# Class biases in four column tiles, vectors laid ready as operands, and a first block in a set order of TensorE

## The chip, the cores and the metric

The kernel runs on one core of a Trainium2 chip. Its time is the device time of one execution in microseconds (us). The kernel before took 2043.91 us, the median of three runs (2043.42 to 2048.09). The profile shows one further execution. The engines are named as in the profile: PE is TensorE, with PEld for its weight loads; DVE is VectorE, ACT is ScalarE, POOL is GpSimd, and SP is SyncE, which here only issues DMAs.

## The reference

Two sequences (B = 2) of 2048 tokens with 512 channels go through three stages, each of which takes the one before as its input:

```python
y   = cond(x, cond_512)                    # a modulated 512x512 linear, clipped
x   = x + attn(y)                          # gated linear recurrence, then a gated MLP with down projection
x   = x + ffn(cond2(x, ids, states))       # six branches, an MLP of two layers, an int8 product
```

The change lies at the seam between the second and the third. What matters there is the first layer of `cond2`:

```python
h = _ln(x, pw_g[pathway_ids], pw_b[pathway_ids]); h = _ln(h, cp_g[compartment_ids], cp_b[compartment_ids])
t = _ln(x, tm_g[time_steps], tm_b[time_steps])
m = x + _mlp_ln(memory_state, ...);  n = x + _mlp_ln(noise_state, ...);  r = x + _mlp_ln(resource_state, ...)
s = _ln(x, ms_g[scale_type], ms_b[scale_type])
cat = concatenate([w[0]*h, w[1]*t, w[2]*m, w[3]*n, w[4]*r, w[5]*s])     # 6 x 512 columns
return _mlp_ln(cat, int_W1, int_b1, int_W2, int_b2, int_g, int_be)      # silu(cat @ int_W1 + b1) @ int_W2 ...
```

Three facts make this cheaper than six products of 512x512. The branches m, n and r all hold the same x plus one vector per sequence, so the blocks of `int_W1` that belong to them are added up, and the three vectors times their blocks become a bias. The ids of a token take few values (5, 3 and 2 classes, 10 in all), so what the additive halves of the class tables contribute after `int_W1` is a table of 10 biases of 512 numbers; a token's own row is picked by a matmul with its one-hot vector. The multiplicative halves (gains) are picked in the same way and multiplied in.

## The kernel before

**Down projection.** The MLP's down projection (`down`) runs over four super-blocks of 1024 tokens. Each is a product of 1536 by 512 in Strassen-Winograd form with seven part products, which `paired_in_place` (L174) sets out: it keeps four quarters of the input, B11, B21, B12, B22, and replaces them by their differences in place (`sums`, L201, DVE). Each part product is a step of PE matmuls (`product`, L129, the matmul at L132): `dn_a` with B11, `dn_b` with B21, `dn_d` with B22 and again with the changed B11, then `dn_a` with the changed B22, with B12 and with B21. One fp32 matmul is two instructions in the records of PE. The changed B22 comes from a difference on DVE, which has to be there before its `dn_a`. Results are added to the residual (L818 and L826 on DVE) and stored. `then` hangs further work behind a step.

**Weights of the third stage.** While the last super-block runs, `int_W1` is made ready. Blocks 3 and 4 lie whole in `int_w_3` and `int_w_4` (`raw`, L1101), blocks 2 and 1 in quarters in two tiles `w_int` (`quarters`, L1107); each block is scaled by its softmax weight (`scaled`, L1083, the scaling at L1085 on DVE). Behind step 1, `vectors_and_x` (L1127) does the following. `vectors` (L1087) multiplies the three vectors by blocks 2, 3 and 4: 12 matmuls of 32 columns by 512, which are put into four column tiles, each with an operand of 128x32 that is set to zero (L1094) and filled by a copy of two columns (L1095) on DVE; four such buffers take turns. The result is copied to `bias` (L1099). POOL adds blocks 3 and 4 onto block 2 (L1131), makes the combinations that the seven products need (`combine`, L119 to L124), and SP loads blocks 5 and 0 (L1115) into the two buffers that blocks 3 and 4 leave; DVE scales them, POOL combines them.

**First block of the third stage.** The third stage works on 8 blocks of 512 tokens. `by_tokens` (L1251) turns x to tokens in rows (`tr_x`, L1266; `tr_oh` for one-hot vectors, L1276), computes layer norms, gathers the rows of `pw` by index (L1246, POOL), multiplies and adds (L1291, L1292) and normalises again; `by_channels` (L1301) turns the normed x (`tr_l`) and the branch h (`tr_h`) back (L1226, with an ACT copy at L1229) to `lnT` and `hT`; `gains` (L1308) picks the gains by a matmul (L1318) and multiplies on DVE (L1323): `tT` and `lnT` both come from `lnT`, then `hT` is multiplied in place. `up` (L1329) then is again `paired_in_place`, with the quarters made of `x2T`, `lnT`, `tT` and `hT`; its banks are `ps_h_a`, `ps_h_b`, `ps_h_d`. `added` (L1359) adds each token's row of the bias table to three of its results.

**Class bias.** Ahead of the first block the table of biases is made (L1498 to L1521): one matmul that brings the sum of the vectors in (L1501), 8 matmuls with an operand of 10 columns (`betas`) in `ps_bias` (L1504) and 4 in `ps_bias_s` (L1510), all 512 long and one behind the other. DVE adds them up (L1517 to L1520), POOL's `split` (L997) cuts the sum into three bf16 parts, and SP stores these as `tables` (L1004).

**Order.** Outside an order written by hand, a scheduler places the instructions of each engine by its own estimates and priorities; once placed, each engine's queue runs in its order, and a waiting instruction holds up all that stand behind it. `tc.manual_schedule` sets an engine's order as written, and `issue_after` puts an instruction behind another on its queue. The gathers of the second block are queued behind the last copy of `split`.

## Time and profile before

| What | us |
|---|---|
| Median of three runs (lowest, highest) | 2043.91 (2043.42, 2048.09) |
| The profiled execution, by its own time | 2045.46 |
| Its span in the profile | 2043.7 |
| PE busy | 2016.0 |
| `ps_vec` and the four dn_d instructions among it | 1341.57 to 1351.20 |
| Class bias on PE, 26 instructions | 1403.86 to 1415.11 |
| First block, from there to its last `added` | 1415.11 to 1443.05 |
| DVE, ACT, POOL busy | 1195.5, 653.2, 157.9 |

The span is the time between the first and last instruction that the profile shows; 1.76 us lie around it. Times along the span count from its start. A timeline lists, for one engine, start and length of groups of like instructions, and in brackets how long the engine had been idle before them and what ended that. The length of a group of PE instructions includes the drain of the last one, so the next can start some 0.17 us before it ends. PEclk is the share of the full TensorE clock that was granted.

### The profile page before, as it was taken

To read this page: it belongs to the slowest core of one execution; us is meant where nothing else is said; L and a number is where in the kernel's file an instruction comes from. 1 tells how busy PE (TensorE), PEld (TensorE's weight loads), DVE (VectorE), ACT (ScalarE), POOL (GpSimd) and SP (SyncE) were. 2 spreads that over 40 slices of the span, in tenths; PEclk is the share of its full clock that TensorE was granted. 3 is DMA by queue.
4 is the path that set the end of the run, shared out by engine and by line. 5 is a ranking of instruction groups with operands and counts; after the bars stand their busy time and mean duration, and the time that the engine had idled before them with its cause. 6 is when DMAs were issued, how large, how long until landed. Compare 5 with 4: busy or idle time off the path is not lost.

```text
span 2043.7 us, 17016 instructions
## 1 busy us (share of the span) xinstructions
PE 2016.0 (99%) x6374; PEld 1067.9 (52%) x6374; DVE 1195.5 (58%) x1798; ACT 653.2 (32%) x861; POOL 157.9 (8%) x126
## 2 busy tenths in 40 slices
PE   8999999999999999999999999999999999999997
PEld 4444444444444444444444444434877777777774
DVE  6766666667533324234325475476588678678675
ACT  4547777776422222222221000001302302302301
POOL 1420000012100000000010000072000000000000
PEclk9999999999999999999999999999999999999999
DMA  6731213232212212111335766624111111111000
GB/s 214 260 136 52 83 52 95 60 113 82 93 42 76 78 41 93 41 42 52 102 116 179 225 223 216 220 94 165 41 43 62 60 45 62 61 43 62 21 21 21
DMA packets 83971, 193.54 MB, mean 95 GB/s; under 512 B 6544, under 2 KB 34742, under 8 KB 79792
## 3 DMA queue, kind: packets, MB, share of 16 engines
q1 hardware_dynamic: 79280, 175.67, 25.3%
q0 software_dynamic: 4608, 16.78, 2.5%
q8 instruction: 50, 0.82, 0.2%
q14 instruction: 33, 0.27, 0.0%
HBM read 133.27 MB, written 58.75 MB: 94 GB/s over the span
## 4 chain that ended last, share of the span: by engine, by line
PE 93%; DVE 4%; DMA 1%; issue 1%; ACT 0%; SPq 0%; DVEq 0%; ACTq 0%
PE up_a L132 16%; PE ps_h_a L132 11%; PE rec_a L132 10%; PE up_d L132 8%; PE dn_a L132 7%; PE ps_h_d L132 6%; PE rec_d L132 5%; PE ps_o L1397 5%; PE up_b L132 4%; PE dn_d L132 4%; PE ps_h_b L132 3%; PE rec_b L132 3%; PE y_a L132 2%; PE dn_b L132 2%; PE ps_f L1421 1%; PE y_d L132 1%
## 5 line engine op out<-in xcount | busy, mean ns | idle before, releaser
L132 PE MATMUL up_a<-h,w_up 128*128 128x512 f32 x384 | 172.6, 592 | 0.0
L132 PE MATMUL dn_a<-op,w_dn 128*128 128x512 f32 x384 | 167.4, 594 | 0.0
L699 DVE SCALAR_TENSOR_TENSOR prod<-up_d,cols,k 128x512 f32<-128x512 f32 x48 | 36.0, 751 | 200.7 <-ACT k L265 200.7
L265 ACT COPY k<-up_a 128x512 f32<-128x512 f32 x144 | 84.2, 585 | 195.4 <-PE up_a L132 195.4
L679 ACT ACTIVATE gate<-gate,cols 128x512 f32<-128x512 f32 x96 | 68.8, 721 | 218.3 <-DVE gate L678 218.3
L132 PE MATMUL up_a<-h2T,w_up 128*128 128x512 f32 x288 | 129.5, 592 | 0.0
L132 PEld LDWEIGHTS up_a<-h,w_up 128*128 128x128 f32 x384 | 72.9, 190 | 91.9 <-issue 89.7
L132 PEld LDWEIGHTS dn_a<-op,w_dn 128*128 128x128 f32 x384 | 72.2, 190 | 88.8 <-issue 86.5
L132 PE MATMUL rec_a<-hT,w_rec 128*128 128x512 f32 x256 | 115.6, 593 | 1.1 <-ACT k L265 1.1
L132 PE MATMUL rec_a<-h,w_rec 128*128 128x512 f32 x256 | 115.1, 592 | 0.0
L1397 PE MATMUL ps_o<-int_w,h 128*128 128x512 f32 x224 | 103.6, 605 | 0.0
L132 PEld LDWEIGHTS up_a<-h2T,w_up 128*128 128x128 f32 x288 | 54.7, 190 | 68.9 <-issue 68.9
L132 PE MATMUL up_d<-h,w_up 128*128 128x512 f32 x192 | 87.5, 599 | 0.0
L132 PE MATMUL up_b<-h,w_up 128*128 128x512 f32 x192 | 86.3, 592 | 0.0
L132 PE MATMUL dn_d<-op,w_dn 128*128 128x512 f32 x192 | 84.2, 595 | 0.0
L132 PEld LDWEIGHTS rec_a<-hT,w_rec 128*128 128x128 f32 x256 | 48.5, 190 | 63.0 <-issue 60.3
L132 PEld LDWEIGHTS rec_a<-h,w_rec 128*128 128x128 f32 x256 | 48.6, 190 | 61.2 <-issue 61.2
L265 ACT COPY k<-rec_a 128x512 f32<-128x512 f32 x96 | 55.7, 580 | 70.2 <-PE rec_a L132 70.0
L678 DVE TENSOR_TENSOR gate<-up_b,k 128x512 f32<-128x512 f32 x48 | 32.9, 690 | 76.1 <-PE up_b L132 74.7
L132 PE MATMUL up_d<-h2T,w_up 128*128 128x512 f32 x144 | 65.2, 592 | 0.0
L1397 PEld LDWEIGHTS ps_o<-int_w,h 128*128 128x128 f32 x224 | 40.2, 189 | 46.5 <-issue 46.5
L132 PE MATMUL ps_h_a<-tT,w_int 128*128 128x256 f32 x256 | 64.2, 385 | 0.0
(389 smaller groups left out, 3475.4 us busy)
## 6 DMA issues: line engine op xcount, KB each, us to landing
pp_d<-prod SPq DMA_DIRECT2D x48, 512.0 KB
op<-pp_d SPq DMA_DIRECT2D x16, 1536.0 KB
x<-in_xT SPq DMA_DIRECT2D x4, 2048.0 KB
y_d<-y SPq DMA_DIRECT2D x16, 512.0 KB
h<-y_d SPq DMA_DIRECT2D x4, 2048.0 KB
yr<-y_d SPq DMA_DIRECT2D x16, 512.0 KB
hs_d<-yr SPq DMA_DIRECT2D x16, 512.0 KB
h<-hs_d SPq DMA_DIRECT2D x4, 2048.0 KB
```

The costliest lines, as they stand in the source:

```text
L132: ins = nc.tensor.matmul(ps, ws[k // 2][:, slot, k % 2, ts(u, P)], xs[k], start=(first and k == 0), stop=(last and k == n - 1), skip_group ...
L265: nc.scalar.copy(t, ps)
L678: nc.vector.tensor_add(gate[u][:, half], ps, kept)
L679: nc.scalar.activation(gate[u][:, half], gate[u][:, half], AF.Gelu, bias=col("L0_attn_mlp_gate_b", fs[u]),)
L699: nc.vector.scalar_tensor_tensor(prod[u][:, b_], ps, col("L0_attn_mlp_fc_b", fs[u]), kept, ALU.add, ALU.add)
L1397: nc.tensor.matmul(ps, h1[:, c, ts(j, P)], w2[:, c, :], start=(c == 0), stop=(c == C - 1))
L1421: nc.tensor.matmul(ps, qT[:, ts(c, P)], rq[:, c, :], start=(c == 0), stop=(c == C - 1))
```

## The change

`vectors` no longer builds its operands: `vectors_as_operands` lays all twelve down beforehand in a padded, zeroed part of the tile of `int_w_3`, so that the 12 matmuls need no DVE instruction between them. The class bias uses operands of 32 columns (the 10 of one class set and what lies next to them), so that its 12 matmuls go to four column tiles of 32 partitions in three groups of four. Their four partial sums in the partitions are added by one matmul, `ps_bias_sum`, with `bias` added first; ACT copies `ps_bias_s` and later the sum. The tile `betas` gets 22 columns more for this.

For block 0 alone, PE's order is set by hand from `tr_l` to the second step of `up`. The first two steps of `paired_in_place` are cut into halves of their inputs (`late`): first half for both u, then second half for both u; the order on PE is tr_oh, tr_l, bias matmuls, gain 1, `ps_h_a` with `x2T`, gain 0, `ps_h_a` with `tT`, tr_h, `ps_h_b` with `lnT` (u = 0), gain 2, `ps_h_b` with `lnT` (u = 1), `ps_bias_sum`, `ps_h_b` with `hT`, `ps_h_d`, and only then the two `added` for `ps_h_b` and `ps_h_d`. `tT` and `lnT` swap their parts in that block. `mids` hands out the last instruction of u = 0 of a step, and the second run of `tr_x` of block 0 is queued behind that of step 5 instead of behind the end of the step. `c11` puts `out11` and its `added` behind `ps_h_d` in that block. From block 1 on, PE, ACT, DVE, POOL and SP have the orders of before.

```diff
     def paired_in_place(ws, B11, B21, B12, B22, banks, tap, out11, out12, out21, out22,
-                        then=(), added=None, shared=False):
+                        then=(), added=None, shared=False, late=None):
 
...
 
         def step(ps, slot, X, first, last):
             X = [x[:, k, :] for x in X for k in range(x.shape[1])]
-            for u in U:
-                ins = product(ps[u], ws, slot, X, u, first and not (u and shared), last)
-                if (step.n, u) in then:
-                    then[step.n, u]()
+            if late and step.n < 2:
+                n = len(ws) // 2
+                for h in (0, 1):
+                    for u in U:
+                        ins = product(
+                            ps[u], ws[n * h : n * h + n], slot, X[2 * n * h : 2 * n * h + 2 * n], u,
+                            first and not h and not (u and shared), last and h,
+                        )
+                        if (step.n, u, h) in then:
+                            then[step.n, u, h]()
+                mids.append(ins)
+            else:
+                for u in U:
+                    ins = product(ps[u], ws, slot, X, u, first and not (u and shared), last)
+                    if not u:
+                        mids.append(ins)
+                    if (step.n, u) in then:
+                        then[step.n, u]()
             ends.append(ins)
             if step.n in then:
                 then[step.n]()
             step.n += 1
 
         step.n = 0
-        ends = []
+        ends, mids = [], []
 
         def sums(out, x, y):
             for t, p, q in zip(out, x, y):
...
 
         pa = banks("a")
         step(pa, 0, B11, True, False)
-        k1 = tap(1, pa, None)
+        with late(0) if late else nullcontext():
+            k1 = tap(1, pa, None)
         pb = banks("b")
-        sums(B11, B12, B11)
-        sums(B12, B22, B12)
-        step(pb, 1, B21, True, not added)
-        more(1, pb)
-        out11(pb, k1)
+        if late:
+            step(pb, 1, B21, True, not added)
+        with late(1) if late else nullcontext():
+            sums(B11, B12, B11)
+            sums(B12, B22, B12)
+        if not late:
+            step(pb, 1, B21, True, not added)
+        def c11():
+            more(1, pb)
+            out11(pb, k1)
+        if not late:
+            c11()
         pd = banks("d")
         step(pd, 6, B22, True, False)
+        if late:
+            c11()
         more(2, pd)
         kd = tap(4, pd, None)
         sums(B22, B22, B11)
...
         step(pa, 3, B21, False, not added)
         more(4, pa)
         out21(pa)
-        return ends
+        return ends, mids
...
-    betas = w3.tile([P, 3, C, R], FP, name="betas", bufs=1)
+    betas_flat = w3.tile([P, 3 * C * R + G - R], FP, name="betas", bufs=1)
+    betas = betas_flat[:, : 3 * C * R].rearrange("p (m c r) -> p m c r", c=C, r=R)
...
 
     def load_classes():
         t = held["cls"] = w14("classes")
-        nc.vector.memset(betas, 0.0)
+        nc.vector.memset(betas_flat, 0.0)
         nc.vector.memset(t[:R, 0:3, :], 0.0)
         for k, (n, lo, m) in enumerate(TABLES):
             nc.sync.dma_start(t[lo : lo + m, k, :], a[n][:, 0:D])
...
         ps = mm("ps_vec")
         for m, rhs in enumerate(of):
             for c in range(C):
-                lhsT = small.tile([P, G], FP, tag="vec", name=f"vec_{m}_{c}", bufs=4)
-                nc.vector.memset(lhsT, 0.0)
-                nc.vector.tensor_copy(lhsT[:, 8:10], vs[m][:, c, :])
                 nc.tensor.matmul(
-                    ps[G * c : G * c + G], lhsT, rhs(c), start=(m == 0), stop=(m == 2)
+                    ps[G * c : G * c + G], held["vec"][:, m, c, :], rhs(c),
+                    start=(m == 0), stop=(m == 2),
                 )
         nc.vector.tensor_copy(bias, ps)
 
     def raw(k):
-        w = w8(f"int_w1_{k}")
-        nc.sync.dma_start(w, block_of(k))
+        w = w14(f"int_w1_{k}")
+        nc.sync.dma_start(w[:, 0:C], block_of(k))
         scaled(k, lambda c: w[:, c, :])
         return w
...
             scaled(k, views[-1])
         return ws, views[0]
 
+    def vectors_as_operands(w):
+        v = padded(w, 3 * C).rearrange("p (m c) g -> p m c g", c=C)
+        for m in range(3):
+            nc.vector.tensor_copy(v[:, m, :, 8:10], vs[m])
+        held["vec"] = v
     w3_4 = [raw(3), raw(4)]
+    vectors_as_operands(w3_4[0])
     w_int, of_x = quarters(2, 1)
     of_34 = [lambda c, w=w: w[:, c, :] for w in w3_4]
...
-    ends = down(NS - 1, {1: vectors_and_x, 2: hand_over})
+    ends, mids = down(NS - 1, {1: vectors_and_x, 2: hand_over})
...
     def stats(mv, j, t, name):
         st = small.tile([P, 6], FP, tag="st", name=f"{name}_st_{j}", bufs=4)
         nc.vector.bn_stats(st, t)
-        nc.vector.bn_aggr(mv[:, j, :], st)
+        held["stats"] = nc.vector.bn_aggr(mv[:, j, :], st)
 
     def rstd_of(mv, name):
         n = mv.shape[1]
         r = small.tile([P, J], FP, tag="rstd", name=f"{name}_rstd", bufs=4)[:, :n]
         v = small.tile([P, 2, J], FP, tag="rv", name=f"{name}_rv", bufs=4)[:, :, :n]
         nc.vector.tensor_scalar(v[:, 0, :], mv[:, :, 1], 1e-5, None, ALU.add)
-        nc.scalar.activation(r, v[:, 0, :], AF.Sqrt)
+        held["root"] = nc.scalar.activation(r, v[:, 0, :], AF.Sqrt)
         nc.vector.reciprocal(r, r)
         refine(r, v[:, 0, :], v[:, 1, :])
         return r
...
         return {"x2T": x2T}
 
     def gather(t, g):
-        with tc.issue_after(tables_done.ins) if J <= t < 2 * J else nullcontext():
+        with tc.issue_after(tables_done[0].ins) if J <= t < 2 * J else nullcontext():
...
             last = normed(t, t, mv2, r, j)
         return last
 
+    def norm_by_channels(i, k):
+        for q in PAIRS:
+            to_channels(block("lnT", i), q, k["ln"][q], f"tr_l_{i}_{q}")
+    def branch_by_channels(i, k):
+        for q in PAIRS:
+            to_channels(block("hT", i), q, k["h0"][q], f"tr_h_{i}_{q}")
     def by_channels(i, k):
-        lnT, hT = k["lnT"], k["hT"] = block("lnT", i), block("hT", i)
-        for q in PAIRS:
-            to_channels(lnT, q, k["ln"][q], f"tr_l_{i}_{q}")
-        for q in PAIRS:
-            to_channels(hT, q, k["h0"][q], f"tr_h_{i}_{q}")
+        norm_by_channels(i, k)
+        branch_by_channels(i, k)
 
     def gains(i, k, n):
 
-        lnT, hT = k["lnT"], k["hT"]
-        if n == 0:
-            k["tT"] = block("tT")
-        dst, src = ((k["tT"], lnT), (lnT, lnT), (hT, hT))[n]
+        if n == 2:
+            dst = src = block("hT", i)
+        else:
+            src = block("lnT", i)
+            dst = block("tT") if n == (not i) else src
         ps = [tr(f"gain_{i}_{n}_{q}") for q in PAIRS]
         for c in range(C):
             of = slice(G * c, G * c + 3 * R)
...
                 start=True, stop=True,
             )
         for q in PAIRS:
-            nc.vector.tensor_mul(duo(dst, q), ps[q], duo(src, q))
+            held["gained"] = nc.vector.tensor_mul(duo(dst, q), ps[q], duo(src, q))
 
     h1s, o4s, mvs = {}, {}, {}
...
     def up(i, k, then):
         h1 = h1s[i] = block("h1")
         h_a, h_b = slice(0, H), slice(H, T)
-        first, second = (k["x2T"], k["lnT"]), (k["tT"], k["hT"])
+        tT, lnT = block("tT"), block("lnT", i)
+        masks, times = (lnT, tT) if i else (tT, lnT)
+        first, second = (k["x2T"], masks), (times, block("hT", i))
 
         def banks(n):
             return m2_ps.tile([P, 2, H], FP, tag="mm", name=f"ps_h1_{i}_{n}").rearrange(
...
 
         paired_in_place(
             w_int, *([t[:, :, h] for t in q] for h in (h_a, h_b) for q in (first, second)),
-            banks, tap, out11, out12, out21, out22, then, added, True,
+            banks, tap, out11, out12, out21, out22, then, added, True, None if i else behind_branch,
         )
 
     def down2(i, nxt):
...
 
     with tc.high_priority():
         k = load(0)
-        normed_h = by_tokens(0, k, ends[4:])
-
-    pb = m2_ps.tile([P, D], FP, tag="mm", name="ps_bias")[:R]
-    pc = m2_ps.tile([P, D], FP, tag="mm", name="ps_bias_s")[:R]
-    n = 0
-    nc.tensor.matmul(pb, summing[:, 0:R], bias, start=True, stop=False)
+        normed_h = by_tokens(0, k, (ends[4], mids[5], ends[6]))
+        branch_stats = held["stats"]
+    first_block = ExitStack()
+    first_block.enter_context(tc.manual_schedule(engines={mybir.EngineType.PE}))
+    norm_by_channels(0, k)
+    pb = m2_ps.tile([P, D], FP, tag="mm", name="ps_bias")
+    pc = m2_ps.tile([P, D], FP, tag="mm", name="ps_bias_s")
+    def beta(m, c):
+        return betas_flat[:, (m * C + c) * R : (m * C + c) * R + G]
     for m, at in ((0, 0), (2, 2)):
         for c in range(C):
             nc.tensor.matmul(
-                pb, betas[:, m, c, :], w_int[at + c // 2][:, 1:4:2, c % 2, :],
-                start=False, stop=(n == 2 * C - 1),
-            )
-            n += 1
+                pb[G * c : G * c + G], beta(m, c), w_int[at + c // 2][:, 1:4:2, c % 2, :],
+                start=(m == 0), stop=(m == 2),
+            )
     for c in range(C):
         nc.tensor.matmul(
-            pc, betas[:, 1, c, :], w_int[2 + c // 2][:, 0:3:2, c % 2, :],
-            start=(c == 0), stop=(c == C - 1),
+            pc[G * c : G * c + G], beta(1, c), w_int[2 + c // 2][:, 0:3:2, c % 2, :],
+            start=True, stop=True,
         )
-
-    with tc.issue_after(normed_h.ins):
-        bias = bias[:R]
-        nc.vector.tensor_copy(bias, pb)
-        for k_ in (0, 1):
-            nc.vector.tensor_add(bias[:, ts(k_, 2 * P)], pc[:, 0 : 2 * P], bias[:, ts(k_, 2 * P)])
-        nc.vector.tensor_sub(bias[:, 2 * P :], bias[:, 2 * P :], pc[:, 2 * P :])
-        tables_done = split(3, bias, [place(f"tab{n % 2}", D, dtype=BF)[:R] for n in range(3)], nc.gpsimd)
-    by_channels(0, k)
-    for n in range(3):
-        gains(0, k, n)
+    def class_sums():
+        pcs = places["k1"]
+        nc.scalar.copy(pcs, pc)
+        lower, upper = slice(0, 2 * P), slice(2 * P, D)
+        with tc.issue_after(normed_h.ins):
+            nc.vector.tensor_add(bias, pb, bias)
+            for of in (lower, upper):
+                nc.vector.tensor_add(bias[:, of], bias[:, of], pcs[:, lower])
+            nc.vector.tensor_sub(bias[:, upper], bias[:, upper], pcs[:, upper])
+    def class_bias():
+        ps = m2_ps.tile([P, D], FP, tag="mm", name="ps_bias_sum")[:R]
+        nc.tensor.matmul(ps, summing[:, 0:R], bias, start=True, stop=True)
+        t = bias[:R]
+        nc.scalar.copy(t, ps)
+        return split(3, t, [place(f"tab{n % 2}", D, dtype=BF)[:R] for n in range(3)], nc.gpsimd)
+    with tc.issue_after(branch_stats.ins):
+        gains(0, k, 1)
+    def times():
+        with tc.issue_after(normed_h.ins):
+            gains(0, k, 0)
+    def behind_branch(n):
+        return tc.issue_after(held["gained"].ins if n else held["root"].ins)
+    tables_done = []
+    in_first = {
+        (0, 1, 0): steps(times, class_sums),
+        (0, 1, 1): lambda: branch_by_channels(0, k),
+        (1, 0, 0): lambda: gains(0, k, 2),
+        (1, 1, 0): lambda: tables_done.append(class_bias()),
+        1: first_block.close,
+    }
     last = None
     for i in range(NB):
         nxt = load(i + 1) if i + 1 < NB else None
-        then = {}
+        then = {} if last else in_first
         if last:
             qs = []
             then[0] = lambda: qs.append(last_norm(i - 1))
```

More of the change, by code (lines that the diff above doesn't have):

```diff
@@ L780, in w14 @@
         return part(w3.tile([P, 7, 2, 2 * P], FP, tag="w", name=name), 7, D)
-    def w8(name):
-        return w14(name)[:, 0:C]
     def tmp(name):
```

## The prediction

> **What bounds the kernel now.** I read the busy shares first, then the span in slices, then the chain around the change, then PE and DVE in order of time.
>
> From the page, shares and slices:
>
> ```profile
> PE 2016.0 (99%) x6374; PEld 1067.9 (52%) x6374; DVE 1195.5 (58%) x1798; ACT 653.2 (32%) x861; POOL 157.9 (8%) x126
> PEclk9999999999999999999999999999999999999999
> ```
>
> PE is the bound, at full clock: other engines matter only where they make PE wait. From the chain of waits between 1335 and 1445 us (start, length, what):
>
> ```profile
> 1350.22 1.05 PE ps_vec L1096 x2
> 1351.27 19.08 PE dn_d L132 x44
> 1370.35 10.30 PE dn_a L132 x24
> ...
> 1403.92 0.96 PE ps_bias L1501 x2
> 1404.88 6.87 PE ps_bias L1504 x16
> 1411.75 3.43 PE ps_bias_s L1510 x8
> ```
>
> The class bias is 0.96 + 6.87 + 3.43 = 11.26 us of PE work with nothing beside it. From the DVE timeline (start, length, instruction, and in brackets its idle time before):
>
> ```profile
> 1349.01 1.16 DVE L1095 COPY vec<-v 128x2 f32<-128x2 f32 x1
> 1351.31 0.69 DVE L1099 COPY bias<-ps_vec 128x512 f32<-128x512 f32 x1 [1.14 <-PE ps_vec L1096]
> 1351.91 2.36 DVE L1085 TENSOR_SCALAR w_int<-w_int,wsm 128x512 f32<-128x512 f32 x2
> 1356.14 2.18 DVE L1085 TENSOR_SCALAR w_int<-w_int,wsm 128x512 f32<-128x512 f32 x2 [1.86 <-DMA w_int<-in_int_W]
> 1358.24 1.75 DVE L818 TENSOR_TENSOR dk<-res,dk 128x512 f32<-128x512 f32 x1
> 1359.91 5.71 DVE L1085 TENSOR_SCALAR w_int<-w_int,wsm 128x512 f32<-128x512 f32 x4
> 1365.54 4.42 DVE L201 TENSOR_TENSOR op<-op,op 128x3072 f32<-128x3072 f32 x1
> ```
>
> This matters most: the last sum makes B22 for the next dn_a, ends at 1369.96, and PE starts that dn_a at 1370.19. Between ps_vec and dn_a PE and DVE run neck and neck.
>
> **The change, part by part.** Times are those of the trace of before.
>
> *Ready vectors.* The 24 instructions of ps_vec (12 matmuls) lie between 1341.57 and 1351.20, mixed with four of dn_d's 48. In their place stands one run, three groups of four column tiles. The price of a group comes from another matmul of that form, on PE's timeline:
>
> ```profile
> 1188.01 1.92 PE L310 MATMUL ps_sv_r<-state_w 128*32 128x512 f32 x16
> 1189.87 5.42 PE L132 MATMUL dn_d<-op,w_dn 128*128 128x512 f32 x12
> ```
>
> Two groups in 1.86 us, 0.93 a group; three take about 2.75, with four tiles side by side. So ps_vec ends at 1344.3 and dn_d, 48 times 19.08 / 44 = 0.434, or 20.8, at 1365.1 at the latest (0.43 each gives 1364.9), five us sooner. But B22 does not come sooner. The DVE copies that go were not what held it: ahead of the sum stand eight scalings L1085, which wait for DMAs of w_int. SP issues these from 1347.72 on, behind POOL's eight adds L1131:
>
> ```profile
> 1342.76 9.83 POOL L1131 TENSOR_TENSOR w_int<-w_int,int_w 128x512 f32<-128x512 f32 x8 [196.69 <-PE ps_vec L1096]
> ```
>
> POOL starts them when ps_vec's first group is through, in both kernels the first thing behind dn_b; it runs 1.23 an add, then combines that pace DVE (L1085 takes 1.43 beside POOL's 1.44). Order on DVE, POOL and SP there is the same but for the vanished copies. So PE has to wait from about 1365 to 1370.1, "dn_a behind op L201". Saving 4.9 to 5.3, new wait 4.9 to 5.3: sum zero. Bounds: 5 saved, if the scalings have slack that I don't see; zero.
>
> *The clock after this wait.* Before has waits of like size. PE's timeline and the table by windows (length, then PE, PEld, DVE, ACT, POOL busy, PEclk, DMA share, GB/s):
>
> ```profile
> 101.25 0.64 PE L420 MATMUL rms_ps<-sq,ones 128*32 128x256 f32 x8 [1.91 <-DVE sq L406]
> 115.51 5.40 PE L132 MATMUL y_d<-x,w_cond 128*128 128x512 f32 x8 [3.12 <-DVE y L500]
> 120.75 3.60 PE L132 MATMUL rec_a<-h,w_rec 128*128 128x512 f32 x8
> ```
>
> ```profile
> 116.00:120.00 4.00, 4.00 (x7) 1.65 (x6) 3.81 (x6) 2.12 (x3) 0.00 (x0) 0.57 0.61 245
> 532.00:536.00 4.00, 4.00 (x7) 1.71 (x6) 2.89 (x4) 0.00 (x0) 0.00 (x0) 0.62 0.03 13
> ```
>
> After 3.12 us idle, eight matmul instructions took 5.40 where the next eight take 3.60: 1.8 lost. After another wait, of 2.63 us at 529, the clock fell the same way. After 1.91 us nothing was lost. A wait of 5 us will cost one such dip. Bounds: 0 (as after 1.91) and 3.6 (two dips in a row, the wait being longer than either row's); I take 1.6, a little under the rows, as in a longer wait part of the slow stretch can fall into the wait itself.
>
> The Trainium skill, page "TensorE: Matmul & The Clock Gate", states a longer limit: an idle window of some 3.4 us halves the clock, so gaps up to there would be free. The trace's gaps of 3.12 and 2.63 us paid already, so the trace decides; for 5 us both expect a dip, and the rule speaks against this change.
>
> *Class bias in column tiles.* Out go 11.26 us. In come three groups of four, 2.75, and one summing matmul of 512 columns, 0.96 as now (L1501): 7.55 saved, all on PE's path, for PE is busy 13.21 of 13.21 us there and what follows is PE work too. Bounds: the form does not overlap (12 matmuls at 0.86 = 10.3, saving nothing: excluded, as ps_vec's eight instructions take 1.07 now); 8.0, if tile groups follow at 0.86.
>
> *Order of the first block.* It now alternates products and gains:
>
> ```profile
> 1419.25 0.39 PE L1318 MATMUL gain<-zone_C,tables 30*128 30x512 bf16 x2
> 1419.56 0.70 PE L132 MATMUL ps_h_a<-zone_A,w_int 128*128 128x256 f32 x2
> 1420.20 0.39 PE L1318 MATMUL gain<-zone_C,tables 30*128 30x512 bf16 x2
> ```
>
> A product piece behind a gain takes 0.63 to the next start where two at the usual 0.216 take 0.43: 0.2 a switch, in six places. The set order has three: 0.6 saved.
>
> *What the set order may wait for.* Counted from 1403.27: tr_l and biases to about 1408.0, gain 1 and the first half product to 1412.3, gain 0, the second half to 1416.6. DVE's products for tT come behind tr_l's copies on ACT and behind the norms of the branch (branch sums now start 0.87 later, since a tr_x run moved ahead of half a dn_a): they end near 1412.5. ACT copies hT's transposes 1.93 us behind tr_h, which PE covers with lnT's u0 products (1.83). Stalls of 0 to 0.5 in sum; I take 0.2. Cover gone, each would be PE idle one for one.
>
> *Bias to tables.* Before, from the last bias matmul at 1415.11 to the last of three table DMAs landed, 1422.75, are 7.6 us (DVE, POOL's split 1416.47 to 1420.88, SP's issues). Now the chain starts at the summing matmul, near 1423.9, with an ACT copy (0.59) in DVE's place: landed about 1431.5 to 1433. PE's adds L1359, moved behind ps_h_d, want the tables at 1434.4. Hidden, 1.5 to 3 us to spare. The next block's gathers, queued behind POOL's split, come 8 us later, about 1440; block 1 added them near 1457.7 before, 1449.7 now. Hidden.
>
> *DVE, ACT and early work.* The vec memsets and copies go, three 128x256 adds and one 128x512 remain: hidden beside PE. Moved sums (L201, 1.22 each) end near 1428, their step comes at 1435. out11 with its add (0.69) moves behind ps_h_d; behind it on DVE stand four sums of 1.22, done near 1440.6, wanted by the step that came at 1451.89 and now at 1443.9: hidden, with 3 us to spare. The tr_x run that moves takes its ACT copies and DVE statistics with it, five us forward into DVE time that PE's dn_a covers. The padded vectors (one POOL memset, three DVE copies) are made long before, where POOL is 8% busy and PE has its products: nothing.
>
> From block 1 on the orders are the same. Sum: 0 − 1.6 + 7.55 + 0.6 − 0.2 = 6.3 us faster. The profiled execution took 2045.46 (span 2043.7 and 1.76 around it) and would take 2039.2; the median of the runs is 1.55 lower, 2043.91, so 2037.6. About 0.3% (6.1 us) is what a measurement of this kernel can tell from no change.
>
> **The rivals.**
> 1. *No new wait at dn_a.* For it: DVE loses 12 copies of up to 1.17. Against it: the scalings wait for DMA, with 1.86 idle in front. Gain 7.95 + 5 = 13, 2031.
> 2. *A late DVE in the first block*: gain 0, tT and hT in a fixed order, no piece of another product can step in. For it: DVE is busy 10.78 of 13.21 us there, and the branch starts 0.87 later. Two to four us of stalls and 1.6 of the dip leave 3: 2041.
> 3. *Column tiles pay less*, each matmul loading its own weights with fp32 in two passes: 12 at 0.45 is 5.4, gain 6.3 − 2.7: 2040.3. Against: L310.
> 4. *Slower: the tables come late.* PE stands at the first add L1359, everything behind it in the queue too. Chain of bias, ACT, POOL, SP: hidden to 1434.4; each us later is lost. It decides against the change from 6.3 us past that, a landing after 1440.7, when the chain of 7.6 has grown to 16.8. Beside gathers and DVE on POOL's side it may grow, hardly double. At 9.5 us past, for instance, 2047; to be slower by 0.3% it needs 12.4.
>
> **How the numbers follow.** Forecast 0.60; rivals 1 to 4: 0.08, 0.17, 0.06, 0.09. The forecast's own range, from the dip (0 to 3.6), the tiles and stalls, is 2035.5 to 2040. Leaving out rival 1 and half of rival 4, with some of the outer rest, gives 2033.5 to 2042.5 for 8 in 10. The bound for faster lies at 2037.8, in the middle of the forecast: 0.35 of its 0.60 and rival 1 are faster by 0.3% (0.43); the rest of it and rivals 2 and 3 within (0.48); rival 4 with its tail, slower (0.09).
>
> **What would show it.** ps_vec in one run of about 2.75 us; PE idle some 5 us ahead of a dn_a, put down to op L201, with PEclk near 0.6 behind it; the bias pieces 2.75 us; no wait over 0.5 at gains and tr_h; first adds at about 1434 to 1437. Wrong if dn_a starts before 1368 without idle, if the clock stays at 1.00, or if PE waits at an add or a gain for a microsecond or more.

## The result

The changed kernel took 2041.32 us, the median of 22 runs (2036.63 to 2045.55), against 2043.91 for the kernel before, also the median of 22 (2041.12 to 2048.09). The ratio, formed over the single runs, is 0.9981, with a 95% interval of 0.9974 to 0.9987: 3.9 us faster, 2.7 to 5.3 (the two medians differ by 2.6). The prediction was 2037.6, with a range of 2033.5 to 2042.5. The range holds the time and the sign is right; the gain is smaller than the 6.3 us forecast and stays within the 0.3% that I had set as the limit of what one measurement tells from no change.

The profiled execution took 2041.97, with a span of 2040.2. PE is still the bound, but it has a new wait. From the page of after, the shares and the clock by slices, and the group of `dn_a` with its idle time:

```profile
PE 2009.0 (98%) x6366; PEld 1069.2 (52%) x6374; DVE 1189.3 (58%) x1777; ACT 654.8 (32%) x863; POOL 164.3 (8%) x127
PEclk9999999999999999999999999999999999999998
L132 PE MATMUL dn_a<-op,w_dn 128*128 128x512 f32 x384 | 169.8, 601 | 5.2 <-DVE op L218 5.2
```

From PE's timeline of after around the change (start, length, instructions, idle before and what ended it). L121 to L132 are as before; `ps_vec` is now L1121, the sums L218, the bias matmuls L1555 and L1560, the summing matmul L1577, gains L1358, PE's adds of the table L1402:

```profile
1343.60 1.06 PE L1121 MATMUL ps_vec<-w_int,int_w 128*32 128x512 f32 x8
1344.49 1.04 PE L1121 MATMUL ps_vec<-int_w 128*32 128x512 f32 x8
1345.35 1.04 PE L1121 MATMUL ps_vec<-int_w,int_w 128*32 128x512 f32 x8
1346.32 20.87 PE L132 MATMUL dn_d<-op,w_dn 128*128 128x512 f32 x48
1372.41 12.89 PE L132 MATMUL dn_a<-op,w_dn 128*128 128x512 f32 x24 [5.23 <-DVE op L218]
...
1409.82 1.93 PE L1555 MATMUL ps_bias<-w_int,betas 128*32 128x512 f32 x16
1411.56 1.04 PE L1560 MATMUL ps_bias_s<-w_int,betas 128*32 128x512 f32 x8
...
1417.38 0.39 PE L1358 MATMUL gain<-zone_C,tables 30*128 30x512 bf16 x2 [0.47 <-DVE tT L1363]
...
1427.27 1.03 PE L1577 MATMUL ps_bias_sum<-bias,sums 128*10 128x512 f32 x2
...
1438.79 0.39 PE L1402 MATMUL ps_h_b<-zone_C,tables 30*128 30x256 bf16 x2
```

The same place on PE's timeline of before, where no wait stands:

```profile
1351.20 19.15 PE L132 MATMUL dn_d<-op,w_dn 128*128 128x512 f32 x44
1370.19 10.46 PE L132 MATMUL dn_a<-op,w_dn 128*128 128x512 f32 x24
```

The parts look as the prediction described them; only PE's first adds come later, at 1438.79 and not at 1434 to 1437, 2 us of it because the whole stretch starts later. `ps_vec` is one run of 2.72 us. The 5 us that it gives back are idle time 21 us later, put down to the sum on DVE. Behind it `dn_a`, 24 instructions, takes 12.89 us where it took 10.46. The bias pieces take 2.72 (1409.82 to 1412.54), and the summing matmul 0.96 later on, where the class bias took 11.25 in all. The clock over the wait and over the slow `dn_a`, from the table by windows of after (length, then busy time of PE, PEld, DVE, ACT, POOL; PEclk; DMA share; GB/s):

```profile
1370.00:1374.00 4.00, 1.59 (x2) 0.84 (x3) 4.00 (x3) 0.00 (x0) 4.00 (x2) 0.54 0.19 27
1374.00:1378.00 4.00, 4.00 (x7) 1.69 (x6) 4.00 (x2) 0.00 (x0) 4.00 (x2) 0.61 0.57 236
1378.00:1382.00 4.00, 4.00 (x11) 1.75 (x10) 1.75 (x3) 0.00 (x0) 3.92 (x3) 1.00 0.01 2
```

And what PE waited for, the DVE timeline of after:

```profile
1354.19 2.50 DVE L1113 TENSOR_SCALAR w_int<-w_int,wsm 128x512 f32<-128x512 f32 x2 [7.05 <-DMA w_int<-in_int_W]
1358.67 2.05 DVE L1113 TENSOR_SCALAR w_int<-w_int,wsm 128x512 f32<-128x512 f32 x2 [1.98 <-DMA w_int<-in_int_W]
1360.65 1.75 DVE L846 TENSOR_TENSOR dk<-res,dk 128x512 f32<-128x512 f32 x1
1362.32 5.70 DVE L1113 TENSOR_SCALAR w_int<-w_int,wsm 128x512 f32<-128x512 f32 x4
1367.94 4.41 DVE L218 TENSOR_TENSOR op<-op,op 128x3072 f32<-128x3072 f32 x1
```

Without its copies DVE now sits idle for 7.05 us, waits for the same DMAs, and ends the sum at 1372.35: 28.75 us behind the start of `ps_vec`, where before it was 28.39 (1369.96 less 1341.57).

A single time holds much that the change does not touch, so I read every profile by four marks on PE: the start of `ps_vec`, the first `dn_a` behind it, `tr_oh`, and the first `tr_x` behind the first block's `ps_h_d` (the next block's). The differences of these starts, in us:

| Kernel | start of ps_vec | ps_vec to dn_a | dn_a to tr_oh | tr_oh to end of block 0 | the three together |
|---|---|---|---|---|---|
| before | 1341.57 | 28.62 | 32.74 | 40.11 | 101.47 |
| after | 1343.60 | 28.81 | 35.17 | 31.74 | 95.72 |

So the profiled execution of after gains 5.75 us over the stretch that the change touches and starts it 2.03 later, though ahead of it only a handful of short DVE and POOL instructions differ. From the second block's `tr_x` to the end of the last matmul it is 595.80 in before and 595.83 in after.

### The profile page after: what moved, and what is told of

Read it like the earlier page. It is cut to its first block, busy times and chain, and to the rows that moved or that the text cites. A ratio compares the mean times of both kernels' runs of the same rounds, so it can differ in the third digit from the quotient of the medians.

```text
span 2040.2 us, 16986 instructions
## 1 busy us (share of the span) xinstructions
PE 2009.0 (98%) x6366; PEld 1069.2 (52%) x6374; DVE 1189.3 (58%) x1777; ACT 654.8 (32%) x863; POOL 164.3 (8%) x127
## 4 chain that ended last, share of the span: by engine, by line
PE 92%; DVE 4%; issue 2%; POOL 1%; DMA 1%; ACT 0%; SPq 0%; POOLq 0%; DVEq 0%; ACTq 0%
PE up_a L132 16%; PE ps_h_a L132 11%; PE rec_a L132 10%; PE up_d L132 8%; PE dn_a L132 7%; PE ps_h_d L132 6%; PE rec_d L132 5%; PE ps_o L1440 5%; PE up_b L132 4%; PE dn_d L132 3%; PE ps_h_b L132 3%; PE rec_b L132 3%; PE dn_b L132 2%; PE y_a L132 2%; PE ps_f L1464 1%
## 5 line engine op out<-in xcount | busy, mean ns | idle before, releaser
L132 PE MATMUL dn_a<-op,w_dn 128*128 128x512 f32 x384 | 169.8, 601 | 5.2 <-DVE op L218 5.2
L132 PE MATMUL up_a<-h,w_up 128*128 128x512 f32 x384 | 172.6, 592 | 0.0
L132 PE MATMUL up_a<-h2T,w_up 128*128 128x512 f32 x288 | 129.5, 592 | 0.0
L132 PEld LDWEIGHTS dn_a<-op,w_dn 128*128 128x128 f32 x384 | 73.0, 193 | 95.7 <-issue 87.8
L132 PEld LDWEIGHTS up_a<-h,w_up 128*128 128x128 f32 x384 | 72.9, 190 | 91.8 <-issue 89.7
L132 PE MATMUL rec_a<-hT,w_rec 128*128 128x512 f32 x256 | 115.5, 593 | 0.7 <-ACT k L293 0.7
L132 PE MATMUL rec_a<-h,w_rec 128*128 128x512 f32 x256 | 115.1, 592 | 0.0
L132 PEld LDWEIGHTS up_a<-h2T,w_up 128*128 128x128 f32 x288 | 54.7, 190 | 68.9 <-issue 68.9
L132 PE MATMUL up_b<-h,w_up 128*128 128x512 f32 x192 | 86.3, 592 | 0.0
L132 PE MATMUL up_d<-h,w_up 128*128 128x512 f32 x192 | 86.3, 592 | 0.0
L132 PE MATMUL dn_d<-op,w_dn 128*128 128x512 f32 x192 | 83.7, 594 | 0.0
L132 PEld LDWEIGHTS rec_a<-hT,w_rec 128*128 128x128 f32 x256 | 48.5, 190 | 62.5 <-issue 60.3
L132 PEld LDWEIGHTS rec_a<-h,w_rec 128*128 128x128 f32 x256 | 48.6, 190 | 61.4 <-issue 61.2
L132 PE MATMUL up_d<-h2T,w_up 128*128 128x512 f32 x144 | 65.2, 592 | 0.0
L132 PE MATMUL ps_h_a<-tT,w_int 128*128 128x256 f32 x256 | 63.9, 385 | 0.0
```

The lines of the kernel that those rows point to most:

```text
L132: ins = nc.tensor.matmul(ps, ws[k // 2][:, slot, k % 2, ts(u, P)], xs[k], start=(first and k == 0), stop=(last and k == n - 1), skip_group ...
```

## The experiments

Each kernel was profiled, and all but one were timed against the kernel before in turns. The marks of all of them are in a table at the end of this section.

### The changed kernel again, and the kernel before again

No edit.

> The changed kernel, unaltered, measured a second time beside the kernel before. Theory (my working, set against the first profile of after): 8.4 us saved between tr_oh and the first block's end, and a half-speed stretch behind the 5.2 us wait at dn_a that costs 0.7 to 3.4 us depending on where it falls, so 5.0 to 7.5 us faster on average, 2036.5 to 2039. Rival: the 22 runs' 3.4 to 3.9 us is the true mean, and then some 2 to 3 us are lost at a place that the one profile does not show. In the profile the start of ps_vec should scatter by 1 to 3 us against before (1341.57) and after (1343.60) if the stretches before the change only differ from execution to execution.

> The kernel before, profiled once more. The stretch from ps_vec's start to dn_a should be 28.6 to 29.6 us, as long as the sum on DVE allows, the two later ones 32.74 and 40.1 us with PE busy throughout; the start of ps_vec, where no kernel here differs, should lie anywhere between 1339 and 1346.

The changed kernel's ratio was 0.9976 (0.9963 to 0.9988), 4.9 us faster with an interval of 2.5 to 7.6. Over the touched stretch its profile shows 95.86 us, and before's second profile 101.91, so that two profiles of each give 5.6 to 6.2 us of gain. The first term came out differently than in the first profile: PE was idle for 6.17 us, and `dn_a` to `tr_oh` took 1.6 us more than in before instead of 2.4. In the kernel before, too, `ps_vec` to `dn_a` was 28.62 once and 29.05 once. The start of `ps_vec` was 1341.31 in after and 1345.45 in before, so that scatter is not the change's.

### The parts apart: tiles and set order alone, ready vectors alone

The first undoes the ready vectors in the changed kernel, the second makes them the only edit to the kernel before:

```diff
 # tiles_only, against the changed kernel
+                lhsT = small.tile([P, G], FP, tag="vec", name=f"vec_{m}_{c}", bufs=4)
+                nc.vector.memset(lhsT, 0.0)
+                nc.vector.tensor_copy(lhsT[:, 8:10], vs[m][:, c, :])
                 nc.tensor.matmul(
-                    ps[G * c : G * c + G], held["vec"][:, m, c, :], rhs(c),
+                    ps[G * c : G * c + G], lhsT, rhs(c),
...
-    vectors_as_operands(w3_4[0])
 # ready_only, against the kernel before: the same lines the other way round
```

> The column-tiled biases and the set order of the first block, but the vectors' operands built on DVE among ps_vec's matmuls, as before. Theory: nothing is lost by that, because the ready vectors only turn dn_d's time into a wait: PE is busy without a gap from ps_vec to dn_a, no half-speed stretch follows, and the whole 8.0 to 8.4 us of the second stretch remain: 2035.5 to 2036, faster than after by the price of the stretch, 0.7 to 3.4 us. Rival (ready vectors are worth their 5 us): slower than after by 3 to 5 us, 2044 to 2046.

> The kernel before with the ready vectors alone. Theory: ps_vec in one run of 2.7 us, PE idle some 5.2 us ahead of dn_a for the sum at L201, a half-speed stretch behind it, and the time of before plus that stretch: 0.7 to 3.4 us slower, 2044.6 to 2047.3. Rival: 5 us faster, 2039.

Measured: tiles alone 0.9956 (0.9940 to 0.9971) of the kernel before, 9.0 us faster (5.9 to 12.3; 7.2 over the touched stretch of the profile), by the middle values more than the whole change brings (3.9 and 4.9); ready vectors alone 1.0003 (0.9993 to 1.0014), no gain at all. PE's timeline of the kernel with the ready vectors alone:

```profile
1345.10 20.87 PE L132 MATMUL dn_d<-op,w_dn 128*128 128x512 f32 x48
1372.05 12.25 PE L132 MATMUL dn_a<-op,w_dn 128*128 128x512 f32 x24 [6.09 <-DVE op L201]
```

and of the one with tiles alone:

```profile
1349.04 19.15 PE L132 MATMUL dn_d<-op,w_dn 128*128 128x512 f32 x44
1368.03 10.46 PE L132 MATMUL dn_a<-op,w_dn 128*128 128x512 f32 x24
```

The wait and the slow `dn_a` come and go with the ready vectors, whatever the first block does. In the profiles they cost 104.32 less 101.47 or 101.91, so 2.9 or 2.4 us. The times alone don't show this cost: ready vectors alone were 0.6 us slower, with an interval from 1.4 faster to 2.9 slower. The rival that they are worth 5 us has fallen by both.

### The sum ahead of the scalings

In the changed kernel the eight scalings of the last two blocks of `int_W1` go behind the sum that makes B22 on DVE's queue; their DMAs are issued as before:

```diff
             for t, p, q in zip(out, x, y):
-                nc.vector.tensor_sub(t, p, q)
+                held["sum"] = nc.vector.tensor_sub(t, p, q)
...
-        ws, _ = quarters(5, 0)
+        w_int.extend(quarters(5, 0, True))          # DMAs only
+    def scaled_behind_sum():
+        views, ws = w_int.pop(), w_int.pop()
+        with tc.issue_after(held["sum"].ins):
+            for k, of in zip((5, 0), views):
+                scaled(k, of)
         for w in ws:
             combine(w)
         w_int.extend(ws)
...
-    ends, mids = down(NS - 1, {1: vectors_and_x, 2: hand_over})
+    ends, mids = down(NS - 1, {1: vectors_and_x, 2: hand_over, 3: scaled_behind_sum})
```

> The changed kernel with the eight scalings of int_W1's last two blocks put behind the sum that makes B22 on DVE's queue. Theory: that sum then waits only for dn_d's reading of its input, ends near 1361.5, and PE goes from dn_d to dn_a without a gap and at full clock: the 5.2 us of the wait and the 0.7 to 3.4 us behind it come on top of after's gain, so 13 to 14 us faster than before, 2030 to 2031. Scalings and combinations end some 5 us later, near 1390, needed at 1405. Rival (something else, such as a PSUM bank or a DMA, is late next): the wait shrinks to 2 us or more, 2034 or above.

> The changed kernel with the eight scalings behind the sum on DVE's queue, measured once more, for a firmer ratio: 12 to 13.5 us faster than before, as its segments (23.4, 32.75, 32.3 us) against before's (28.6 to 29.1, 32.74, 40.1) say. PE without a wait at dn_a, with a clock of 1.00 there, whatever the start of ps_vec.

Measured: 2033.95 and 2032.05 us, ratios 0.9939 (0.9921 to 0.9957) and 0.9935 (0.9920 to 0.9950): 12.5 to 13.3 us faster than before. It beats both kernels. DVE and PE of the second run:

```profile
1354.35 4.26 DVE L218 TENSOR_TENSOR op<-op,op 128x3072 f32<-128x3072 f32 x1 [3.75 <-PE dn_d L132]
1358.53 10.31 DVE L1113 TENSOR_SCALAR w_int<-w_int,wsm 128x512 f32<-128x512 f32 x8
1368.77 4.42 DVE L218 TENSOR_TENSOR op<-op,op 128x3072 f32<-128x3072 f32 x1
```

```profile
1343.74 20.87 PE L132 MATMUL dn_d<-op,w_dn 128*128 128x512 f32 x48
1364.45 10.46 PE L132 MATMUL dn_a<-op,w_dn 128*128 128x512 f32 x24
```

The sum now waits for PE's reading of its input alone and ends at 1358.6, six us before PE wants it. `ps_vec` to `dn_a` is 23.42 us in both runs, 5.2 less than before. What is late next are the gains, 1.3 us in the second run (0.5 and 0.8, for DVE's `tT`; 1.0 in the first). The chain that the trace draws from there goes back through DVE's work on the branch h to its gather: DVE was idle for 7.62 us before it.

### The same order on DVE without ready vectors

The same edit, made in the kernel with the tiles alone.

> Scalings behind the sum, as in that kernel, but the vectors' operands built on DVE among the matmuls of ps_vec. Tells apart whether the order on DVE is worth something by itself. Theory: no, since PE then is the one that comes last at dn_a: ps_vec to dn_a takes 28.6 us, the time is that of the kernel with the tiles alone, 7 to 8.5 us faster than before. So neither of the two edits shortens this stretch alone, both together do by 5.2 to 5.6. Rival (the order on DVE brings the gain): 23.4 to 26 us there, and 10 us or more faster than before.

Measured: 0.9961 (0.9945 to 0.9976), 8.0 us faster (4.9 to 11.2), and 29.91 us from `ps_vec` to `dn_a`, without a wait at `dn_a`. There PE is late by itself, held up for 2.1 us by DVE's copies and memsets among `ps_vec`, 1.3 us more in all than I had put. So it takes both edits: PE's way through `ps_vec` and the sum's way through DVE were of one length, and only when both are shortened does the stretch get shorter.

### The wait filled with work

Extra matmuls, whose result nobody reads, behind `dn_d` and ahead of the `dn_a` that waits; five, then seven. `hand_over`, which hands PSUM banks on, moves behind them:

```diff
+    def keep_warm():
+        with tc.issue_after(held["step"].ins):        # the last matmul of dn_d
+            ps = mm("ps_warm")
+            for n in range(5):                        # warm_full: 7
+                nc.tensor.matmul(
+                    ps, ones, w_dn[0][:, 0, :, :].rearrange("p h o -> p (h o)"),
+                    start=(n == 0), stop=(n == 4),
+                )
+        hand_over()
-    ends, mids = down(NS - 1, {1: vectors_and_x, 2: hand_over})
+    ends, mids = down(NS - 1, {1: vectors_and_x, 3: keep_warm})
```

> The changed kernel with five extra 128x512 matmuls (4.3 us of PE work whose result nobody reads) in the wait ahead of dn_a. Theory: PE stays idle for only 0.9 to 1.9 us, dn_a starts when it did (28.8 to 29.8 us behind ps_vec's start), and the half-speed stretch is gone: dn_a to tr_oh takes 32.7 us as before and not 34.4 to 35.2, so 1.6 to 2.4 us faster than after, 2038 to 2039. Rival (the longer dn_a has another cause, such as POOL and DVE working on the same memory): 34.4 to 35.2 us again, and the time of after.

> The changed kernel with seven extra 128x512 matmuls (6.0 us, result unread) in the wait ahead of dn_a, where five left 1.92 us idle and the half-speed stretch came all the same (dn_a to tr_oh 34.55 us, clock 0.50 to 0.66). Theory: the stretch hangs on idle time inside a fixed interval of about 3.4 us, and 1.92 was enough for it; with PE busy up to within 0.5 us of the sum's end the clock stays at 1.00 and dn_a to tr_oh takes 32.74 us, as before. dn_a starts up to 0.8 us later than the sum allows. Net against after: 1 to 2 us faster. Rival (clock falls for another reason at this place): 34.4 us or more again.

With five the ratio was 0.9975 (0.9963 to 0.9987), that of the changed kernel; with seven 0.9964 (0.9952 to 0.9977). PE with five, and the clock:

```profile
1366.75 4.46 PE L1186 MATMUL ps_warm<-w_dn,ones 128*128 128x512 f32 x10
1373.13 12.26 PE L132 MATMUL dn_a<-op,w_dn 128*128 128x512 f32 x24 [1.92 <-DVE op L219]
```

```profile
1373.00:1375.00 2.00, 1.87 (x3) 0.97 (x4) 2.00 (x3) 0.00 (x0) 2.00 (x2) 0.66 0.37 86
1375.00:1377.00 2.00, 2.00 (x3) 0.68 (x2) 2.00 (x1) 0.00 (x0) 2.00 (x2) 0.50 0.94 389
```

and with seven:

```profile
1363.99 6.17 PE L1186 MATMUL ps_warm<-w_dn,ones 128*128 128x512 f32 x14
1370.00 10.46 PE L132 MATMUL dn_a<-op,w_dn 128*128 128x512 f32 x24
```

My expectation of the first failed: 1.92 us of idle time brought the stretch of half clock as 5 and 6 us had, and it cost 1.8 us. The second shows that idle time is its cause. DVE and POOL work beside `dn_a` as ever, the clock is 1.00, and `dn_a` to `tr_oh` is back at 32.74. In the profiles 6 us of useless PE work make this kernel 1.5 us shorter over the touched stretch than after (94.22 against 95.72), though `dn_a` now starts 0.8 us later than the sum on DVE would let it. The intervals of the two ratios overlap.

### The bias in one tile

All twelve bias matmuls go to the first column tile; DVE and ACT add up that tile's 32 rows. The order stays.

```diff
-                pb[G * c : G * c + G], beta(m, c), w_int[at + c // 2][:, 1:4:2, c % 2, :],
-                start=(m == 0), stop=(m == 2),
+                pb[:G], beta(m, c), w_int[at + c // 2][:, 1:4:2, c % 2, :],
+                start=(m == 0 and c == 0), stop=(m == 2 and c == C - 1),
...
-            pc[G * c : G * c + G], beta(1, c), w_int[2 + c // 2][:, 0:3:2, c % 2, :],
-            start=True, stop=True,
+            pc[:G], beta(1, c), w_int[2 + c // 2][:, 0:3:2, c % 2, :],
+            start=(c == 0), stop=(c == C - 1),
```

> The changed kernel, with the 12 bias matmuls all in the first column tile, one behind the other, and the sums over the four tiles made on that tile alone; order and all else as changed. Theory: each matmul of 32 columns by 512 takes 0.86, as the 10-column ones did, so the twelve take 10.3 us where three groups take 2.75: 7.5 us slower than after, all of it in the stretch from tr_oh to the end of block 0 (39.3 us against 31.75). DVE is then early and the 0.5 us at the gains goes: 7 to 7.5. Rival (the set order and the halves bring a good part of the 8.4 us): 3 to 5 us slower.

Measured: 1.0007 (0.9996 to 1.0018) of the kernel before. From its PE timeline:

```profile
1408.53 7.05 PE L1555 MATMUL ps_bias<-w_int,betas 128*32 128x512 f32 x16
1415.42 3.60 PE L1560 MATMUL ps_bias_s<-w_int,betas 128*32 128x512 f32 x8
1418.94 0.40 PE L1358 MATMUL gain<-zone_C,tables 30*128 30x512 bf16 x4
```

The twelve take 10.41 us where three groups of four take 2.72. The first block takes 39.07 us against 31.74: the tiles are worth 7.3 us. What is left between 39.07 and before's 40.11, 1.0 us, is the set order with the halves, a stall of 0.30 at the gains already taken off. The rival that the order brings 3 to 5 us has fallen.

### The summing matmul later

```diff
-        (1, 1, 0): lambda: tables_done.append(class_bias()),
+        (1, 1, 1): lambda: tables_done.append(class_bias()),
```

> The changed kernel with the summing matmul behind the second half of ps_h_b (hT), 3.55 us later, instead of ahead of it. This tests the cover of the bias tables, which I had put at 1.5 to 3 us. In the profiles of after the last table lands at the very moment PE wants it (PE's adds start 0.1 us late), because POOL's split took 7.2 us instead of 4.4. Theory: no cover is left, so PE stands about 3 to 3.7 us ahead of the adds, and the time is 3 to 3.7 us longer than after, with a half-speed stretch of 0 to 2 us on top. Rival (the split is faster when DVE's sums are done by then, so it catches up): 0.5 to 2 us.

Measured: 0.9974 (0.9963 to 0.9986), and 31.92 us for the first block: nothing is lost. Both of my expectations were too high, and the first rested on a misreading. The 0.1 us ahead of PE's adds is no wait: the kernel before has the same 0.11 there, at its changes from fp32 to bf16. And the rival's reason holds fully. POOL's split in after:

```profile
1428.98 1.64 POOL L1028 CAST tab<-bias 10x512 bf16<-10x512 f32 x1 [26.30 <-ACT bias L1579]
1430.70 2.01 POOL L1030 TENSOR_TENSOR bias<-bias,tab 10x512 f32<-10x512 f32 x1
1432.77 1.49 POOL L1028 CAST tab<-bias 10x512 bf16<-10x512 f32 x1
1434.33 1.14 POOL L1030 TENSOR_TENSOR bias<-bias,tab 10x512 f32<-10x512 f32 x1
1435.54 0.60 POOL L1028 CAST tab<-bias 10x512 bf16<-10x512 f32 x1
```

and with the summing matmul later:

```profile
1433.01 0.60 POOL L1028 CAST tab<-bias 10x512 bf16<-10x512 f32 x1 [29.92 <-ACT bias L1579]
1433.69 1.15 POOL L1030 TENSOR_TENSOR bias<-bias,tab 10x512 f32<-10x512 f32 x1
1434.91 0.60 POOL L1028 CAST tab<-bias 10x512 bf16<-10x512 f32 x1
1435.59 1.15 POOL L1030 TENSOR_TENSOR bias<-bias,tab 10x512 f32<-10x512 f32 x1
1436.80 0.60 POOL L1028 CAST tab<-bias 10x512 bf16<-10x512 f32 x1
```

In after the split runs beside DVE's sums of two tensors (L218 until 1433.79) and takes 7.2 us, to 1436.14; when it starts behind them, it takes 4.4, to 1437.40. Counted from PE's first add, its end moved from 2.65 us ahead (1438.79) to 2.0 us ahead (1439.40), by 0.65 and not by the 3.55 of the matmul. The last update that tells of the third table's landing stands at 1438.05 in after's trace and at 1439.31 in this one's: after had 0.7 us of cover, and this kernel 0.1.

### All marks

| Kernel | start of ps_vec | ps_vec to dn_a (idle in it) | dn_a to tr_oh | tr_oh to end of block 0 | together |
|---|---|---|---|---|---|
| before | 1341.57 | 28.62 | 32.74 | 40.11 | 101.47 |
| before, again | 1345.45 | 29.05 | 32.75 | 40.12 | 101.91 |
| after | 1343.60 | 28.81 (5.23) | 35.17 | 31.74 | 95.72 |
| after, again | 1341.31 | 29.75 (6.17) | 34.35 | 31.77 | 95.86 |
| ready vectors alone | 1342.38 | 29.67 (6.09) | 34.53 | 40.12 | 104.32 |
| tiles and order alone | 1339.12 | 28.91 | 32.74 | 32.64 | 94.30 |
| sum first | 1345.43 | 23.42 | 32.75 | 32.31 | 88.48 |
| sum first, again | 1341.03 | 23.42 | 32.74 | 32.67 | 88.83 |
| sum first, operands built | 1338.00 | 29.91 | 32.74 | 32.24 | 94.90 |
| five extra matmuls | 1343.34 | 29.79 (1.92) | 34.55 | 32.12 | 96.46 |
| seven extra matmuls | 1340.57 | 29.43 | 32.74 | 32.05 | 94.22 |
| bias in one tile | 1342.61 | 28.37 (4.79) | 35.31 | 39.07 | 102.75 |
| summing matmul later | 1344.24 | 28.86 (5.28) | 34.90 | 31.92 | 95.68 |

## Why the prediction was right, and where it was off

The sum was 0 − 1.6 + 7.55 + 0.6 − 0.2 = 6.3. The profile's 5.75 is −0.2 − 2.4 + 7.3 + 1.0: the errors of the terms partly cancel, which is luck. Nor does the number alone speak for the forecast: 2041.32 lies outside its own range of 2035.5 to 2040 and beside rival 2's 2041; it is the profiles that tell them apart. Term by term:

- **Ready vectors, 0.** Right in mechanism: the saving turned into a wait for the sum. In size it was −0.2 and −1.1 in the two profiles against before's first, and +0.2 and −0.7 against its second. The end of the sum follows the length of POOL's eight adds, whichever kernel it is: 28.3 to 28.4 us behind the start of `ps_vec` where they took 9.8 (before, and one tile, which has the ready vectors), 28.8 where they took 10.3 (after, and before again), 29.7 where they took 11.0 (after, again). So a loss by the ready vectors themselves isn't shown; nor had my lower bound of zero a reason that excludes one.
- **The dip, −1.6.** The behaviour was right; the size was at the low end. Measured against before's 32.74 it was 2.4, 1.6 (after), 1.8 (ready vectors alone), 2.6 (one tile) and 2.2 (summing matmul later) in the five profiles that wait for 4.8 to 6.2 us, 2.1 on average. The traces' records of the granted clock give the size: in all five the stretch at half clock is 6.83 us long, twice that behind the waits of 3.12 and 2.63 us in before, and begins inside the wait. The part of it that falls behind the wait, 4.7, 3.1, 3.4, 5.0 and 4.2 us, costs half its length, 2.4, 1.5, 1.7, 2.5 and 2.1. So part of the stretch does fall into the wait, as I had argued, but it was the two dips in a row of my outer bound. From the start of `ps_vec` to `tr_oh` the ready vectors thus cost 2.2 to 2.8 us in the profiles.
- **Column tiles, +7.55.** 7.3, by the kernel with one tile.
- **Set order, +0.6 − 0.2.** 1.0 where 0.4 stood. The stall was about as large as its bound, 0.47 at the second gain where I had put 0 to 0.5, so the order must bring more than the 0.6 of three switches, 1.3 with the one-tile kernel's stall of 0.30. Where the rest comes from was not measured by itself.
- **Bias to tables, hidden.** Hidden, but with 0.7 us of cover where I had put 1.5 to 3, since POOL's split took 7.2 us and not 4.4. The rival that this chain comes late was thus closer than I had thought, and did not come about.
- **The lower bound of the dip, 0.** This step failed: I took a wait of 1.91 us as one that costs nothing, and 1.92 us cost 1.8 in the kernel with five extra matmuls. The very wait of 1.91 us that I had gone by was followed by half clock in the second profile of after (last section).

Over the touched stretch the gain was 5.6 to 6.2 us in the profiles, near the 6.3. The ratios of the timed runs say 3.9 (2.7 to 5.3) and 4.9 (2.5 to 7.6). The first interval lies just below the profiles, and I can't settle whether the rest of the difference is the changing start of `ps_vec` (1338.0 to 1345.45 over thirteen profiles, with no pattern that I see by the edits) or a loss ahead of it that profiles of single executions don't show. Behind the stretch at most 0.4 us are lost: the span goes on for 600.5 to 600.9 us in twelve of the thirteen profiles (601.8 in the one-tile kernel's). Rival 1, no wait, fell with the first profile; its 13 us were had only with DVE's order changed as well. Rival 2, a late DVE in the first block, has a stall of 0.47 us to show and not two to four. Rival 3, tiles that pay less, fell with the 2.72 us and with the one-tile kernel.

## What to carry to other kernels

Where two engines run neck and neck towards one instruction, shortening one of them alone buys a wait, not time; find the other chain and shorten both, as in the kernel with the sum ahead of the scalings, which took 12.5 to 13.3 us off. A wait on TensorE can cost more than its own length, since a stretch at half clock can follow, which cost 1.6 to 2.6 us here; one that can't be removed is cheaper when filled with work. In an in-order queue, look for what stands ahead of the instruction that everyone waits for and isn't needed yet.

## What the runs showed of the hardware

The length of an idle time alone does not decide whether the clock falls. One and the same wait, at `up_a` near 530 us, left the clock at 1.00 after 2.47 us in after and after 2.02 us in its second profile, and halved it after 2.63 us in before and after 2.41 us in the kernel with five extra matmuls. From PE's timelines and the tables by windows, eight us each around or behind that wait, of before, after and the kernel with five extra matmuls:

```profile
531.62 2.50 PE L132 MATMUL up_a<-hT,w_up 128*128 128x512 f32 x4 [2.63 <-ACT k L265]
531.00:539.00 8.00, 7.38 (x14) 3.15 (x15) 4.46 (x6) 1.29 (x3) 0.00 (x0) 0.79 0.14 58
```

```profile
535.18 1.98 PE L132 MATMUL up_a<-hT,w_up 128*128 128x512 f32 x4 [2.47 <-ACT k L293]
535.00:543.00 8.00, 7.82 (x18) 3.53 (x19) 5.71 (x8) 2.06 (x4) 0.00 (x0) 1.00 0.20 82
```

```profile
532.66 2.54 PE L132 MATMUL up_a<-hT,w_up 128*128 128x512 f32 x4 [2.41 <-ACT k L294]
531.00:539.00 8.00, 6.33 (x11) 2.79 (x12) 4.70 (x7) 1.70 (x3) 0.00 (x0) 0.79 0.16 66
```

The wait of 1.91 us ahead of `rms_ps`, behind which the clock stayed at 1.00 in before, was followed by half clock in the second profile of after:

```profile
103.55 0.64 PE L448 MATMUL rms_ps<-sq,ones 128*32 128x256 f32 x8 [1.91 <-DVE sq L434]
104.00:108.00 4.00, 4.00 (x9) 1.65 (x6) 1.51 (x3) 2.59 (x4) 0.00 (x0) 0.57 0.93 289
```

What decides can be read from the records of the granted clock in the traces. Between 40 and 2015 us, every stretch at half clock in the thirteen traces is 3.41 us long or twice that, and within one trace their starts lie whole multiples of 3.413 us apart: 116.53 and 532.96 in before are 122 of them apart, 117.61 and 1370.30 in after 367. If a trace is cut into intervals of 3.413 us at these marks, then half clock set in behind each of the 25 intervals at full clock in which PE was idle for 1.90 us or more, and behind none with 1.87 or less. The 1.92 us ahead of `dn_a` lay in one interval, 1370.22 to 1373.63; the 2.47 us of after were divided, 1.32 and 1.15. The intervals are read from the positions; what was tested is that half clock is gone when the wait is filled.

The Trainium skill, page "TensorE: Matmul & The Clock Gate", section "Part 1: The HAM clock gate", says that the window of about 3.4 us over which TensorE's activity is judged runs freely and doesn't start anew with the kernel; that fits a wait that counts or not by where it falls. Its limit of a whole idle window does not fit: 1.92 us were enough here.

Four column tiles at once cost hardly more than one: twelve fp32 matmuls of 32 columns by 512 took 2.72 us in three groups of four and 10.41 us in one tile, 3.8 times as long.

POOL's operations of 10 rows by 512 (casts and subtractions) took 1.5 to 2.0 us beside DVE sums of two tensors and 0.60 and 1.15 without them, and such a DVE sum took 2.17 us beside them (at 1431.62 in after) where it takes 1.22 without (at 1431.78 in the kernel with the summing matmul later).
